# Four cross-attention layers on one core: two of eight subtractions move to GpSimd, one bank is ranked last, one product is issued later

## The chip, the core and the metric

The kernel runs on one core of a Trainium2 chip. The metric is device time in microseconds (us) of one execution, without the host. The kernel before takes 3668.16 us, the median of three runs (3667.93 to 3672.54).

## What is computed

Four cross-attention layers run one after the other on four batches. Layers 0, 2 and 3 are alike and are called *masked*: 16 heads of 64, and a bias on a few key columns, which comes from two masks over the queries. Layer 1 is called *grouped*: an RMS norm first, 16 query heads of 16, four key heads.

```python
# masked layer (0, 2, 3); x: (4, 512, 256), context: (4, 1024, 512)
q, k, v = x @ Wq, ctx @ Wk, ctx @ Wv           # 16 heads of 64
logits = einsum('bhqd,bhkd->bhqk', q, k) * 64 ** -0.5 + col_bias
out = einsum('bhqk,bhkd->bhqd', softmax(logits), v) @ Wo + bo + x
# grouped layer (1)
xn = x * rsqrt(mean(x * x) + 1e-5) * norm_w
scores = einsum('btgrd,bsgd->bgrts', q, k) * 0.25
out = einsum('bgrts,bsgd->btgrd', softmax(scores), v) @ wo + x
```

All data are float32.

## The kernel before, in words

**Units and steps.** The work of a layer and a batch is cut into eight units of two heads. There are 96 masked and 32 grouped units. A hand-written table (lines 57 to 64) gives every one of 96 steps one masked unit and, in 32 of them, a grouped one as well. The instruction order of all engines is written out in program order (`manual_schedule`); nothing is reordered afterwards. In the main loop (line 1029) a step `n` knows

- `g`, the masked unit whose logits are made in this step, and `g1`, that of the step before, whose product with the values is made now,
- `lam`, the grouped unit of this step, whose logits were already made in the step before,
- `coming`, the grouped unit of the next step, whose logits are made in this one.

The text calls a step with `coming` and without `lam` a *coming step* (there are 28: 11, 13, 15 ... 23, 27 ... 39 and so on), and one with `lam` a *lam step* (32, of which four, 24, 40, 56 and 72, also have a `coming`). Mostly the two kinds alternate.

**A masked unit.** `scores` (line 695) makes the logits, transposed: eight tiles of 128 keys by 1024 (two heads of 512 queries, one to each half of a tile). Each tile takes one pair of PSUM banks: TensorE multiplies (L704; every float32 product is two matmul records, so a tile has four), ScalarE copies the pair to SBUF (L714), and VectorE takes the running maximum of all eight in the first tile's pair (L718), the unit's `mx_place`. `max_quarters` (line 759) reduces that maximum (L755), gives `mx_place` back, and works on through L765 to L770 in a scratch bank of its own, `w`. `max_everywhere` spreads the result over a pair of banks, `mb` (L781). Then VectorE subtracts `mb` from the eight tiles (L789), ScalarE takes exponentials (L795), GpSimd adds the exponentials up (L834) in `g.mx`, a ninth slot in SBUF beside the unit's eight tiles. In the next step `attend` multiplies with the values (L734), and `normalise` divides (L755 on `st`, L859 to L880).

**A grouped unit.** In the step before, `logits_pair` (line 676) makes its logits in four pairs of tiles, spread between the projections of that step (L681 on TensorE, L687 on ScalarE, L693 on VectorE); after the fourth pair come `max_quarters` and `max_everywhere`, here into SBUF. In its own step GpSimd makes all eight subtractions (L787), before anything else of that step; ScalarE takes the exponentials, and `attend_grouped` (line 1180) makes the product, as one item of the list below.

**The fill list.** After `scores` and `attend`, a step has a list of projections (`fill`, lines 1162 to 1214), each with a cost in us, which TensorE works off while VectorE and ScalarE finish the softmax. The events (subtractions and exponentials, lines 1148 to 1154) are put between the items by these costs, whenever an item that returns a function has been issued. `attend_grouped` goes into the list where the costs ahead of it reach 9.5, and not ahead of an output projection of a grouped unit.

**Banks.** PSUM has eight banks, handed out at build time by `Place` (lines 99 to 121): a `Place(2)` takes the even-odd pair that has been returned longest ago, by a running number of returns, and a `Place(1)` the bank returned longest ago (preferring one whose neighbour is out). So the number written by `back()` decides which bank the next tiles get, and with it whose reads they wait for.

Of the kernel before, what the change touches and what calls it, by code (L numbers as in the profile page):

```python
# [12 lines left out]
ALU = mybir.AluOpType  # L13
# [7 lines left out]
NT = T // P  # L21
# [61 lines left out]
def kernel(ctx: ExitStack, tc: tile.TileContext, a: dict, out: bass.AP):  # L83
    nc = tc.nc
# [8 lines left out]
    def t_(shape, tag, name, bufs=1, dtype=FP):  # L93
        return sb.tile(shape, dtype, tag=tag, name=name, bufs=bufs)
# [40 lines left out]
    def give_set(g):  # L135
        sets_free.append(g.set)
# [501 lines left out]
    def reciprocal_rows(out_, in_, room):  # L638


        turned = room[:, 0:S]
        short = t_([P, S // 32, 1], "short", f"short{len(turns)}")
        turns.append(0)
        nc.vector.transpose(turned, in_)
        nc.vector.reciprocal(short, turned.rearrange("p (c r) -> p c r", r=32)[:, :, 0:1])
        nc.vector.transpose(
            out_.rearrange("p (c r) -> p c r", r=32), short.to_broadcast([P, S // 32, 32])
        )
# [75 lines left out]
    def attend(g, blocks=range(NT)):  # L724
        for t in blocks:
            for j in range(2):
                rows = g.rows[j]
                if not g.masked:
                    rows = slice(64 * g.h + 32 * j, 64 * g.h + 32 * (j + 1))
                at, first, last = rows, 0, NT - 1  # L730
                if not g.masked:
                    at = slice(64 * (t % 2) + 32 * j, 64 * (t % 2) + 32 * (j + 1))
                    first, last = t % 2, NT - 2 + t % 2
                nc.tensor.matmul(  # L734
                    g.po[at, :], lhsT=g.v[:, t, rows], rhs=g.st[t][:, j * S : (j + 1) * S],
                    start=(t == first), stop=(t == last),
                )
# [16 lines left out]
    def over_quarter(out_, of, op):  # L754
        nc.vector.tensor_reduce(  # L755
            out_, of.rearrange("p (b x) -> p b x", x=32), AX.X, op, apply_transpose=True
        )

    def max_quarters(g):
        w = Place(1)  # L760
        quarter, half = w.ap[:, 0:32], w.ap[0:64, 32:64]
        other = t_([64, 32], "other_max", f"other_max_{g.name}")
        over_quarter(quarter, g.mx_place.ap, ALU.max)
        g.mx_place.back()
        nc.vector.tensor_copy(other, quarter[64:128, :])  # L765
        nc.vector.tensor_tensor(half, quarter[0:64, :], other, ALU.max)
        nc.vector.tensor_copy(other[0:32, :], half[32:64, :])
        g.every = t_([P, 2 * S // 32, 1], "every", f"every_{g.name}")
        for h in range(4):
            nc.vector.tensor_tensor(  # L770
                g.every[32 * h : 32 * (h + 1), :, 0], half[0:32, :], other[0:32, :], ALU.max
            )
        w.back()

    def max_everywhere(g):
        if g.masked:
            g.mb_place = Place()
            g.mb = g.mb_place.ap
        else:
            g.mb = g.mx  # L780
        nc.vector.transpose(  # L781
            g.mb.rearrange("p (b r) -> p b r", r=32), g.every.to_broadcast([P, 2 * S // 32, 32])
        )

    def subtract(g, t):
        if not g.masked:
            nc.gpsimd.tensor_tensor(g.st[t], g.st[t], g.mb, ALU.subtract)  # L787
            return
        nc.vector.tensor_tensor(g.st[t], g.st[t], g.mb, ALU.subtract)  # L789
        if t == NT - 1:  # L790
            g.mb_place.back()

    def exponentials(g, t):
        st = g.st[t]
        nc.scalar.activation(st, st, AF.Exp)  # L795
        if t == 0 or not g.masked:
            return
        g.acc = g.mx
        if t < g.now:
            running_sum(g, t)  # L800
# [9 lines left out]
    def attend_last(g):  # L810

        place_out(g, 2)
        parts_of = [g.st[t] for t in range(g.now, NT)] + [g.acc]

        def add(n):
            for j in range(2):
                nc.tensor.matmul(
                    g.psum[g.rows[j], :], lhsT=ones[:, 0:64], rhs=parts_of[n][:, j * S : (j + 1) * S],
                    start=(n == 0), stop=(n == NT - g.now),
                )  # L820

        for t in range(NT):
            for j in range(2):
                nc.tensor.matmul(
                    g.po[g.rows[j], :], lhsT=g.v[:, t, g.rows[j]], rhs=g.st[t][:, j * S : (j + 1) * S],
                    start=(t == 0), stop=(t == NT - 1),
                )
            if t >= g.now:
                add(t - g.now)
        add(NT - g.now)  # L830
        g.ot = t_([P, S], "ot", f"ot_{g.name}", bufs=3)
# [41 lines left out]
    def normalise(g):  # L873
        w = Place(1)
        reciprocal_sums(g, w.ap)
        w.back()
        scale_out(g)
# [5 lines left out]
    def project_out(*of):  # L883

        g = of[0]
        x, acc = xs[g.l, g.b], xs.get((g.l + 1, g.b))
        opens = acc is None
        if opens and g.masked:
            acc = new_state(g.l + 1, g.b)
        elif opens:  # L890

            acc = xs[g.l + 1, g.b] = x
            x_at[g.l + 1, g.b] = x_at[g.l, g.b]
        w = Place()
        m = w.ap
        for k in range(KC):
            for each in of:
                nc.tensor.matmul(  # L898
                    m[:, k * S : (k + 1) * S], lhsT=each.wo[:, k * P : (k + 1) * P], rhs=each.ot,
                    start=each is g, stop=each is of[-1],  # L900
                )
        y = m.rearrange("p (k q) -> p k q", q=S)

        def add_last(q):
            nc.vector.tensor_tensor(acc[:, :, q], y[:, :, q], acc[:, :, q], ALU.add)

        def add():
            if g is masked[-1]:
                for i in range(0, NI, 2):
                    add_last(slice(i * P, (i + 2) * P))  # L910
                    store(g.b, range(i, i + 2))
                left[g.b] = -1
            elif opens and g.masked:
                bo = columns[f"L{g.l}_xattn_bo"]
                for k in range(KC):
                    nc.vector.scalar_tensor_tensor(
                        acc[:, k, :], y[:, k, :], bo[:, k : k + 1], x[:, k, :], ALU.add, ALU.add
                    )
            else:
                nc.vector.tensor_tensor(acc, y, x if opens else acc, ALU.add)  # L920
            w.back()

        left[g.b] -= len(of)
        return add
# [33 lines left out]
    def at(n):  # L958
        return steps[n] if 0 <= n < len(steps) else (None, None)
# [8 lines left out]
    def head(g):  # L968
        return steps[step_of[1, g.b, 0]][1]
# [59 lines left out]
    for n in range(len(steps) + 2):  # L1029
        g, lam = at(n)  # L1030
        follows, coming = at(n + 1)
# [99 lines left out]
        if g:  # L1131
            max_quarters(g)
            max_everywhere(g)
        if g1 and g:
            attend(g1)
            give_set(g1)
            if not ending:
                late.append(lambda: normalise(g1))
        elif g1:
            attend_last(g1)  # L1140
            adds = [project_out(*each) for each in outs]
            outs = []
            reciprocal_rows(g1.ot, g1.psum, g1.mx)
            scale_out(g1)
            for add in adds:
                add()
# [8 lines left out]
        if coming:  # L1155
# [6 lines left out]
        fill, of_grouped = (  # L1162
            [
                (1.8 * len(each), lambda each=each: project_out(*each))
                for each in outs if each[0].masked == m
            ]
            for m in (True, False)
        )
# [9 lines left out]
        if lam:  # L1178

            def attend_grouped():  # L1180
                while any(of is lam for _, of, _ in events):
                    events.pop(0)[2]()
                lam.v = head(lam).v
                place_out(lam)
                attend(lam)
                give_set(lam)
                late.append(lambda: keep_odd(lam))
                if lam.h == 1:
                    late.append(lambda: turn_grouped(lam))
                return lambda: keep_even(lam)  # L1190

            total, where = 0.0, 0
            first_at = max((fill.index(each) + 1 for each in of_grouped), default=0)
            while where < len(fill) and (total < 9.5 or where < first_at):
                total += fill[where][0]
                where += 1
            fill.insert(where, (3.6, attend_grouped))
# [79 lines left out]
```

## Time and profile before

| | |
|---|---|
| median of three runs | 3668.16 us |
| the profiled execution, its own time | 3666.02 us |
| its span, first to last instruction | 3664.2 us |
| TensorE matmul, busy | 3550.1 us (97%) |
| VectorE | 3019.4 us (82%) |
| ScalarE | 2317.6 us (63%) |
| GpSimd | 2219.7 us (61%) |
| one subtraction on VectorE (L789), 768 of them | 1215 ns |
| one subtraction on GpSimd (L787), 256 of them | 2376 ns |
| one copy of a pair of banks by ScalarE (L714), 768 | 1044 ns |
| granted TensorE clock, mean | 0.998 |

How to read it: the 97% does not say that TensorE streams all the time. A matmul that waits in the array, or runs beside another at less than full speed, counts as busy, too. A stall is better seen in the times at which the matmuls of one stage start. The `scores` of a step start with its first L704 matmul; that is taken as the start of the step. Step 17 starts at 642.1, step 18 at 682.7, step 19 at 722.6 us. Granted clock and DMA are no limit here (DMA moved 42 GB/s in the mean).

### The profile page before, as it was taken

To read this page: it belongs to the slowest core of one execution; us is meant where nothing else is said; L and a number is where in the kernel's file an instruction comes from. 1 tells how busy PE (TensorE), PEld (TensorE's weight loads), DVE (VectorE), ACT (ScalarE), POOL (GpSimd) and SP (SyncE) were. 2 spreads that over 40 slices of the span, in tenths; PEclk is the share of its full clock that TensorE was granted. 3 is DMA by queue.
4 is the path that set the end of the run, shared out by engine and by line. 5 is a ranking of instruction groups with operands and counts; after the bars stand their busy time and mean duration, and the time that the engine had idled before them with its cause. 6 is when DMAs were issued, how large, how long until landed. Compare 5 with 4: busy or idle time off the path is not lost.

```text
span 3664.2 us, 40591 instructions
## 1 busy us (share of the span) xinstructions
PE 3550.1 (97%) x14510; PEld 1719.1 (47%) x14510; DVE 3019.4 (82%) x4134; ACT 2317.6 (63%) x2657; POOL 2219.7 (61%) x1005
## 2 busy tenths in 40 slices
PE   8999999999999999999999999999999999999998
PEld 4554444444454444444444444444444445454454
DVE  7877788888878878897888889788878978888787
ACT  4556566666756666675666667566666765555554
POOL 3565466656746665684666658556765755545454
PEclk9999999999999999999999999999999999999999
DMA  3231101101021011102101110110002011002100
GB/s 88 61 118 53 55 28 41 31 18 51 19 67 42 26 30 48 57 19 61 49 26 28 55 51 19 53 56 27 28 28 72 19 32 49 18 26 72 32 29 8
DMA packets 164845, 154.69 MB, mean 42 GB/s; under 512 B 42776, under 2 KB 142616, under 8 KB 164132
## 3 DMA queue, kind: packets, MB, share of 16 engines
q1 hardware_dynamic: 158990, 139.00, 12.1%
q0 software_dynamic: 2560, 8.39, 0.7%
q10 hardware_dynamic: 3094, 4.72, 0.6%
q8 instruction: 114, 1.87, 0.2%
q14 instruction: 87, 0.71, 0.1%
HBM read 133.20 MB, written 14.68 MB: 40 GB/s over the span
## 4 chain that ended last, share of the span: by engine, by line
PE 76%; DVE 15%; ACT 6%; issue 2%; ACTq 0%; DMA 0%; DVEq 0%; POOL 0%; POOLq 0%
PE ps L734 16%; PE ps L526 16%; PE ps L565 15%; PE ps L704 15%; PE ps L898 4%; PE ps L622 4%; PE ps L681 4%; DVE ps L718 4%; DVE st L789 3%; ACT st L795 3%; DVE ps L755 2%; DVE ps L693 2%; ACT st L714 2%; ACT st L687 1%; DVE ps L781 1%
## 5 line engine op out<-in xcount | busy, mean ns | idle before, releaser
L834 POOL TENSOR_TENSOR st<-st 128x1024 f32<-128x1024 f32 x668 | 1579.6, 2365 | 1112.6 <-ACT st L795 1067.7
L795 ACT ACTIVATE st<-st 128x1024 f32<-128x1024 f32 x1024 | 1038.3, 1056 | 570.2 <-DVE st L789 499.6
L718 DVE TENSOR_TENSOR ps<-ps,st 128x1024 f32<-128x1024 f32 x672 | 827.6, 1232 | 384.0 <-ACT st L714 323.3
L789 DVE TENSOR_TENSOR st<-st,ps 128x1024 f32<-128x1024 f32 x768 | 881.2, 1215 | 3.3
L734 PE MATMUL ps<-st,v 128*64 128x512 f32 (+1 forms) x4064 | 802.1, 596 | 8.5 <-ACT st L795 8.5
L704 PE MATMUL ps<-qt,kt 64*128 64x512 f32 x3072 | 732.8, 604 | 75.4 <-DVE ps L755 45.2
L714 ACT COPY st<-ps 128x1024 f32<-128x1024 f32 x768 | 718.8, 1044 | 128.4 <-PE ps L710 64.3
L787 POOL TENSOR_TENSOR st<-st 128x1024 f32<-128x1024 f32 x256 | 596.8, 2376 | 295.3 <-DVE st L781 295.3
L526 PE MATMUL ps<-ctx,wk 128*128 128x512 f32 x1536 | 692.4, 600 | 2.2 <-ACT ctx L428 2.2
L565 PE MATMUL ps<-wv,ctx 128*128 128x256 f32 x3072 | 682.3, 381 | 0.0
L565 PEld LDWEIGHTS ps<-wv,ctx 128*128 128x128 f32 x3072 | 581.5, 190 | 130.6 <-issue 53.5
L704 PEld LDWEIGHTS ps<-qt,kt 64*128 64x128 f32 x3072 | 315.6, 187 | 434.9 <-issue 130.3
L734 PEld LDWEIGHTS ps<-st,v 128*64 128x64 f32 (+1 forms) x4064 | 242.2, 130 | 545.0 <-issue 432.3
L526 PEld LDWEIGHTS ps<-ctx,wk 128*128 128x128 f32 x1536 | 285.7, 191 | 394.0 <-issue 369.4
L693 DVE TENSOR_TENSOR ps<-ps,st 128x1024 f32<-128x1024 f32 x224 | 276.1, 1232 | 86.8 <-ACT st L687 75.4
L687 ACT COPY st<-ps 128x1024 f32<-128x1024 f32 x256 | 247.0, 1015 | 87.0 <-PE ps L681 86.6
L572 ACT COPY v<-ps 128x512 f32<-128x512 f32 x192 | 110.5, 576 | 150.9 <-PE ps L565 150.6
L628 ACT ACTIVATE qt<-ps 128x512 f32<-128x512 f32 x96 | 56.6, 590 | 220.2 <-PE ps L622 220.2
L622 PE MATMUL ps<-x,wq 128*128 128x512 f32 x384 | 188.1, 613 | 1.1 <-ACT x L391 1.1
L681 PE MATMUL ps<-qt,kt 32*128 32x512 f32 x1024 | 171.5, 640 | 8.0 <-DVE o L748 5.2
L898 PE MATMUL ps<-ot,wo 128*128 128x512 f32 x384 | 177.9, 606 | 0.7 <-DVE ot L880 0.7
L531 ACT COPY kt<-ps 128x512 f32<-128x512 f32 x192 | 110.8, 577 | 101.5 <-PE ps L526 97.2
(142 smaller groups left out, 1696.4 us busy)
## 6 DMA issues: line engine op xcount, KB each, us to landing
ctx<-kept SPq DMA_DIRECT2D x30, 1024.0 KB, 8.0
wk<-in_L_xattn_Wk_dram SPq DMA_DIRECT2D x47, 512.0 KB, 3.6
wv<-in_L_xattn_Wv_dram SPq DMA_DIRECT2D x47, 512.0 KB, 3.7
wq<-in_L_xattn_Wq_dram SPq DMA_DIRECT2D x96, 128.0 KB, 3.5
wo<-in_L_xattn_Wo_dram SPq DMA_DIRECT2D x96, 128.0 KB, 3.9
st<-kept SPq DMA_DIRECT2D x4, 2048.0 KB
kept<-st SPq DMA_DIRECT2D x12, 512.0 KB, 3.2
qt<-qt ACTq DMA_DIRECT2D x32, 128.0 KB, 2.2
```

The costliest lines, as they stand in the source:

```text
L526: nc.tensor.matmul(m, lhsT=g.w["k"][:, k, :], rhs=ctx_half[g.b, n][:, k, :], start=(k == 0), stop=(k == KT - 1),)
L565: nc.tensor.matmul(m[:, half * 2 * P : (half + 1) * 2 * P], lhsT=ctx_half[g.b, t // 4][:, k, t % 4 * P : (t % 4 + 1) * P], rhs=g.w["v2"][: ...
L622: nc.tensor.matmul(m, lhsT=g.wq[:, k, :], rhs=x[:, k, :], start=(k == 0), stop=(k == KC - 1))
L693: nc.vector.tensor_tensor(top, top, g.st[t], ALU.max)
L704: nc.tensor.matmul(m[:, j * S : (j + 1) * S], lhsT=g.kt[g.rows[j], keys], rhs=g.qt[g.rows[j], :], start=True, stop=t > 0,)
L714: nc.scalar.copy(g.st[t], m)
L718: nc.vector.tensor_tensor(top, top, g.st[t], ALU.max)
L734: nc.tensor.matmul(g.po[at, :], lhsT=g.v[:, t, rows], rhs=g.st[t][:, j * S : (j + 1) * S], start=(t == first), stop=(t == last),)
L787: nc.gpsimd.tensor_tensor(g.st[t], g.st[t], g.mb, ALU.subtract)
L789: nc.vector.tensor_tensor(g.st[t], g.st[t], g.mb, ALU.subtract)
L795: nc.scalar.activation(st, st, AF.Exp)
L834: nc.gpsimd.tensor_tensor(g.acc, g.st[0] if t == 1 else g.acc, g.st[t], ALU.add)
```

## The change

It has three parts.

- **A.** In the 28 coming steps two of the eight masked subtractions (tiles 6 and 7) are made by GpSimd. GpSimd's operand is in SBUF, so ScalarE first copies `mb` from PSUM into `g.mx`, which the running sum overwrites afterwards. The copy and the two subtractions are issued right after `max_everywhere`. `mb` is given back after VectorE's last subtraction, now that of tile 5.
- **B.** In `max_quarters` the pair `mx_place` of a *grouped* unit is given back with a return number that is higher by six. `Place` then ranks it behind the banks that are returned after it.
- **C.** In lam steps without a `coming`, `attend_grouped` goes into the fill list where the costs ahead of it reach 13.0, and no longer 9.5.

```diff
@@ max_quarters
-        g.mx_place.back()
+        g.mx_place.back(0 if g.masked else 6)
@@ subtract
+        if t >= g.here:
+            return
         nc.vector.tensor_tensor(g.st[t], g.st[t], g.mb, ALU.subtract)
-        if t == NT - 1:
+        if t == g.here - 1:
             g.mb_place.back()
+
+    def subtract_aside(g):
+        nc.scalar.copy(g.mx, g.mb)
+        for t in range(g.here, NT):
+            nc.gpsimd.tensor_tensor(g.st[t], g.st[t], g.mx, ALU.subtract)
@@ main loop
             max_quarters(g)
             max_everywhere(g)
+            g.here = NT - 2 if coming and not lam else NT
+            if g.here < NT:
+                subtract_aside(g)
@@ attend_grouped's place
-            while where < len(fill) and (total < 9.5 or where < first_at):
+            while where < len(fill) and (total < (9.5 if coming else 13.0) or where < first_at):
```

## The prediction

> **What bounds the kernel now.** I read the page's busy shares first, then the list of who waited for whom, then the timeline around the start of one lam step.
>
> ```profile
> PE 3550.1 (97%) x14510; PEld 1719.1 (47%) x14510; DVE 3019.4 (82%) x4134; ACT 2317.6 (63%) x2657; POOL 2219.7 (61%) x1005
> ```
>
> TensorE (PE) is busy by far the longest, so relief for VectorE (DVE) counts only where TensorE waits for it. From the list of waits (who waited, for whom, total us, times, longest; PEld are TensorE's weight loads):
>
> ```profile
> PE ps L704 <- DVE ps L755: 45.2, 28, 2.1
> PE ps L704 <- ACT st L687: 27.4, 24, 1.2
> PE ps L734 <- ACT st L795: 8.5, 10, 1.2
> ```
> ```profile
> PEld ps L704 <- DVE every L770: 8.7, 28, 0.3
> ```
>
> The logits (L704) wait 28 times for the reduction L755: once in each lam step but the first of each batch (12, 28, 44, 60). The timeline where step 17 ends and step 18 begins (start, duration, engine, line; in brackets the idle time before and its releaser):
>
> ```profile
> 681.62 1.93 ACT L687 COPY st<-ps 128x1024 f32<-128x1024 f32 x2 [0.54 <-PE ps L681]
> 682.66 2.57 DVE L693 TENSOR_TENSOR ps<-ps,st 128x1024 f32<-128x1024 f32 x2 [0.61 <-ACT st L687]
> 682.68 1.13 PE L704 MATMUL ps<-qt,kt 64*128 64x512 f32 x4 [1.14 <-ACT st L687]
> ...
> 683.86 1.02 PE L704 MATMUL ps<-qt,kt 64*128 64x512 f32 x4
> ...
> 685.27 1.26 DVE L755 TRANSPOSE_TENSOR_REDUCE ps<-ps 128x32 f32<-128x1024 f32 x1
> ...
> 686.59 6.02 PE L704 MATMUL ps<-qt,kt 64*128 64x512 f32 x24 [1.70 <-DVE ps L755]
> ...
> 687.23 0.76 DVE L770 TENSOR_TENSOR every<-ps,other_max 32x32 f32<-32x32 f32 x4
> ...
> 689.27 4.68 ACT L714 COPY st<-ps 128x1024 f32<-128x1024 f32 x5 [0.45 <-PE ps L704]
> ```
>
> Tiles 0 and 1 start at 682.68 and 683.86, tile 2 at 686.59, when the grouped L755 has ended. The next stage (L734) starts at 692.54, so the logits took 9.86 us. Where nothing waits (step 19, from 722.63 to 729.92) they take 7.29. So 2.57 us are lost in each of these 28 steps.
>
> **B, the banks.** I followed `Place` by hand through both versions. Before, step 18 takes, tile by tile: the pair of the coming step's last even logits, that of its last odd logits, the grouped `mx_place` (waits for L755), and a fourth pair, one bank of which was `max_quarters`' scratch `w`. That scratch is read last by L770. After, `mx_place` ranks last, so the fourth pair becomes third. Tile 2 then waits not for L755 (ends 686.53) but for L770 (ends 687.99), later in the same DVE chain. In this case at tile 2 only the half on the scratch bank waits. The trace of before shows that this wait is real: the 28 PEld waits for L770 are tile 3's, which was held only 0.3 us, having started late.
>
> Further, `mx_place` now comes up only at tile 7 (or, in some steps, not at all), so tiles 1 to 6 alternate between two pairs and not three. Worked through for step 18: tile 2's second half starts at 688.05. Before, tile 3's second half started then and its copy at 689.27, that is 1.22 later; copies take 0.94 each (4.68/5), a tile of matmuls 0.86 (four records, two at a time, 0.43 apart). So after: tile 2's copy 689.27 to 690.2; tile 3 688.9 to 689.8, copy to 691.1; tile 4 needs tile 2's pair, 690.25, copy 691.5 to 692.4; tile 5 691.2, copy to 693.3; tile 6 needs tile 4's pair, 692.45; tile 7 693.3 to 694.2; L734 at about 694.35. That is 1.8 us later than 692.54: 0.86 for the tile that slipped, the rest for two pairs in place of three. VectorE's maxima hide nothing of it: L734 follows on TensorE at once, and what TensorE loses there stays lost, since its later items in the step wait for nothing else (C's stall apart). All 28 have this order of banks: 28 x 1.8 = +50. The four first lam steps had no wait, but also get fewer pairs in rotation: tile 3 waits 0.6 for tile 1's copy, +2.4. Two plain steps, 26 and 42, start on other banks, freed sooner, about -0.7 each; in six coming steps (29, 39, 45, 55, 61, 71) a logits tile now gets banks that wait for the key copy L531, about +0.3 each. These cancel.
>
> **C, the later product.** Timeline of step 18, TensorE:
>
> ```profile
> 710.09 3.63 PE L734 MATMUL ps<-st,v 128*32 128x512 f32 x28
> 714.55 1.05 PE L734 MATMUL ps<-st,v 128*32 128x512 f32 x4 [0.83 <-ACT st L795]
> ```
>
> The grouped product runs from 710.09 to the next L565 at 715.53: 5.44 us, against 3.57 in step 16. It waits for the last grouped exponentials. In twelve lam steps the starts show this (1.9 to 2.2 us in ten, 1.0 in two: 46 and 54), together 21 us. Listed two value items later, each some 1.7 us (L565: 7.1 us for four), it arrives 3.4 us later by itself and 1.8 more by B, after the exponentials: all 21 go. What stands behind it is late but has cover: the copy L744 and the divisions L748 to L851 ended at 721.7 in step 18, the next step's first maximum starts at 726.0. C: -21.
>
> **A, the subtractions.** Removed: 28 x 2 x 1.215 = 68 us of DVE. Added: 28 copies of 1.04 on ACT (as L714), 56 subtractions of 2.37 on POOL (as L787), 133 us. The timeline of step 17:
>
> ```profile
> 660.62 2.19 ACT L795 ACTIVATE st<-st 128x1024 f32<-128x1024 f32 x2 [9.63 <-DVE st L789]
> ...
> 662.89 9.68 POOL L834 TENSOR_TENSOR st<-st 128x1024 f32<-128x1024 f32 x4 [16.45 <-ACT st L795]
> ...
> 663.90 5.74 DVE L789 TENSOR_TENSOR st<-st,ps 128x1024 f32<-128x1024 f32 x5
> ...
> 667.71 3.02 ACT L795 ACTIVATE st<-st 128x1024 f32<-128x1024 f32 x3
> ...
> 670.64 0.57 ACT L531 COPY kt<-ps 128x512 f32<-128x512 f32 x1
> ```
>
> The ACT copy waits for L781 (ends 659.33), runs to 660.4 and fits in the idle 9.63; the first exponential queues behind it, but waits for the first subtraction until 660.6 anyway. POOL subtracts from 660.5 to 665.3, ahead of ACT's use at 669; the seven sums behind it end 2.4 us later (682.2 for 679.8), before POOL's next job at 689.4. So the added work is hidden. But what is gained? TensorE's first pair of grouped logits waits for L531, and L531 for ACT's three exponentials in a row, bound by ACT itself. The later maxima (L693) wait for L687, not for earlier DVE work (0.61 before the last two, above). So the chain L687, L693, L755, L770 ends when it did. A: 0. If DVE set the end, -68; if the copies stood on the path, +29. The rows stand at nothing. If an ACT copy were no longer covered, 1.04 us a step.
>
> [...] L789 in step 18 takes 9.15 us for eight beside a working POOL, in step 17 3.48 for three beside an idle one: 1.14 and 1.16 each, no slowing. [...]
>
> **Sum.** 3666.0 (the profiled execution) + 50 + 2 - 21 + 0 = 3697 or 3698. The median of the runs lies 2.1 above that execution, so 3700 us, 0.9% slower.
>
> **Rivals.**
>
> - *DVE's chain ends earlier after all* (faster). If A lets L770 end 2.43 us sooner, tile 2 starts at 685.6 and L734 at 691.9, 0.6 before now: 28 x -0.6 - 21 + 2 = -36, 3632. It turns faster from about 1.1 us of advance, where B costs 0.7 a step and C pays it. For it: DVE is freed shortly before L693 begins. Against it: the waits of L693 for L687.
> - *Only the slipped tile costs* (no change). If two pairs in rotation are enough, B is 28 x 0.86 = 24, and with C's -21 the sum is +3 to +5: 3672.
> - *The halves fall out of step* (much slower). In steps 46, 54 and 68 the logits took 1.7 to 1.9 us more than in the other 25: a half that was released alone ran in turn with its neighbour, not beside it. Now a lone half is the rule at tile 2. If it happens in all, 28 x 1.7 = 48 on top: 3748. For the main case: in 25 of 28 it did not.
>
> **How the numbers follow.** Main case 0.62 (its own range 3680 to 3722: B from 1.2 to 2.6 a step), out of step 0.12, no change 0.11, faster 0.15. Range 3650 to 3740: from half of the faster case's gain to most of the out-of-step case; A's far ends, -68 and +29, are kept out beyond that, since no wait in the rows points to them. A measurement of this kernel can tell about 0.2% (7 us) from no change. Chances: faster 0.14, same 0.11, slower 0.75.
>
> **What would show it.** Right: the waits of L704 for L755 gone, and about 28 waits for L770 of some 3 us in their place; L704 in lam steps 11.5 to 11.7 us; no wait of L734 for L795; coming steps as long as before, with six L789 each. Wrong: L755 and L770 earlier after the last L687 than now, shorter coming steps, or tile 2 starting without a wait.

## The result and the profile after

| kernel | median of runs, us | lowest to highest | ratio to before, 95% interval |
|---|---|---|---|
| before, beside the changed kernel | 3668.05 | 3664.66 to 3672.54 | 1 |
| changed (A, B and C) | 3756.61 | 3756.32 to 3760.72 | 1.0243 [1.0226, 1.0261] |

The change makes the kernel 2.4% slower. The sign was forecast; the size, 3700, was not, and 3756.61 lies above the range. The profiled execution took 3760.72 us, its span is 3758.9 (3664.2 before): 94.7 us more.

The page of the changed kernel, busy times:

```profile
PE 3617.8 (96%) x14510; PEld 1708.6 (45%) x14510; DVE 2960.2 (79%) x4078; ACT 2340.8 (62%) x2685; POOL 2350.7 (63%) x1061
```

VectorE has lost 59 us of work, GpSimd has gained 131 with the 56 moved subtractions. (The prediction's 68 for VectorE multiplies the 1.215 us of one; subtractions in a row overlap a little: the five at 663.90 in step 17 of before took 5.74 us, 1.148 each.) TensorE does the same 14510 matmuls, but is busy 67.7 us longer: stalled or slower matmuls, not more of them.

The changed kernel's list of waits (who waited, for whom, total us, times, longest):

```profile
PEld ps L704 <- DVE every L770: 90.2, 28, 4.3
...
PE ps L704 <- DVE every L770: 67.1, 28, 3.5
...
DVE st L791 <- ACT st L796: 30.2, 28, 1.1
...
PE ps L681 <- ACT kt L531: 15.2, 28, 0.9
```

The waits of the logits for L755 are gone. Waits for L770 stand in their place, as the prediction said of part B. The third line was not foreseen. (Part A adds seven lines to the code: the subtraction is now L791, ScalarE's copy L796, GpSimd's subtraction L798, the exponential L802.)

The third line in the timeline of the changed kernel, step 17 (which starts at 650.0; start, duration, engine, line, in brackets the idle time before and its releaser):

```profile
665.59 1.26 DVE L781 STREAM_TRANSPOSE ps<-every 128x1024 f32<-128x1024 f32 x1
666.89 1.01 ACT L796 COPY st<-ps 128x1024 f32<-128x1024 f32 x1 [8.02 <-DVE ps L781]
667.93 3.48 DVE L791 TENSOR_TENSOR st<-st,ps 128x1024 f32<-128x1024 f32 x3 [1.08 <-ACT st L796]
667.98 4.70 POOL L798 TENSOR_TENSOR st<-st 128x1024 f32<-128x1024 f32 x2 [15.65 <-ACT st L796]
669.19 2.19 ACT L802 ACTIVATE st<-st 128x1024 f32<-128x1024 f32 x2 [1.29 <-DVE st L791]
```

L781 has written the maxima into `mb` at 666.85. VectorE idles 1.08 us until ScalarE has read the same `mb`. In step 17 of the kernel before, L781 ended at 659.33 and VectorE went on without a pause:

```profile
659.37 3.48 DVE L789 TENSOR_TENSOR st<-st,ps 128x1024 f32<-128x1024 f32 x3
```

The first exponential, and all that hangs on it, moves by about as much.

The start of lam step 18 in the changed kernel:

```profile
692.35 1.88 PE L704 MATMUL ps<-qt,kt 64*128 64x512 f32 x6
692.56 1.93 ACT L714 COPY st<-ps 128x1024 f32<-128x1024 f32 x2 [0.52 <-PE ps L710]
...
693.76 1.26 DVE L755 TRANSPOSE_TENSOR_REDUCE ps<-ps 128x32 f32<-128x1024 f32 x1
...
695.73 0.77 DVE L770 TENSOR_TENSOR every<-ps,other_max 32x32 f32<-32x32 f32 x4
...
696.55 6.77 PE L704 MATMUL ps<-qt,kt 64*128 64x512 f32 x18 [2.32 <-DVE every L770]
```

The second half of tile 2 starts at 696.55, when L770 has ended, and not after L755. From there to the next stage, at 704.10, 22 matmuls take 7.55 us (the last line shows the first 18 of them). In step 24 of the same kernel the same 22 took 6.38. The windows view of step 18 shows why (window, its length, then the busy times of PE, PEld, DVE, ACT and POOL, the granted TensorE clock, DMA share, GB/s):

```profile
691.20:697.10 5.90, 3.58 (x14) 1.43 (x16) 5.55 (x11) 2.76 (x3) 0.00 (x0) 1.00 0.59 154
697.10:700.50 3.40, 3.40 (x10) 1.40 (x6) 3.03 (x3) 1.61 (x2) 2.58 (x2) 0.51 0.01 2
```

For 3.4 us after the wait the clock is half; step 24 has no such stretch. In the kernel before, the same view of step 46, one of the three odd steps of the prediction's third rival:

```profile
1823.40:1826.80 3.40, 3.40 (x10) 2.65 (x9) 3.29 (x3) 1.56 (x2) 2.25 (x1) 0.50 0.00 0
```

Half clock there, too. The clock records hold 3 such stretches before (10.2 us in all) and 29 after (36 windows of 3.413 us, 122.9 us; the one at the very end, 6.5 us before and 5.6 after, left out). Of the 29, 25 lie in the logits of lam steps and four in the coming steps 27, 29, 39 and 59. So the sentence ahead of the prediction, that the granted clock is no limit, holds for the kernel before alone, and there but for these 10 us.

**Where the 94.7 us are**, by the starts of the stages in both traces: +87.3 in the logits of the 32 lam steps (28 of them from 9.95 to 12.98 us in the mean, the four others from 7.3 to 7.9); +35.4 in the coming steps, between their first grouped logits and their end; -20.8 at the grouped product; -7.1 in small ones (-5.5 at L565 in lam steps with a `coming`, -1.6 in steps 26 and 42).

### The profile page after: what moved, and what is told of

It reads as the page before. It is cut to its first block, busy times and chain, and to the rows that moved or that the text cites. A ratio compares the mean times of both kernels' runs of the same rounds, so it can differ in the third digit from the quotient of the medians.

```text
span 3758.9 us, 40578 instructions
## 1 busy us (share of the span) xinstructions
PE 3617.8 (96%) x14510; PEld 1708.6 (45%) x14510; DVE 2960.2 (79%) x4078; ACT 2340.8 (62%) x2685; POOL 2350.7 (63%) x1061
## 4 chain that ended last, share of the span: by engine, by line
PE 71%; DVE 18%; ACT 7%; issue 3%; DMA 0%; DVEq 0%; ACTq 0%; POOL 0%; POOLq 0%
PE ps L565 18%; PE ps L734 15%; PE ps L704 13%; PE ps L526 12%; DVE ps L718 7%; PE ps L622 4%; PE ps L681 4%; DVE st L791 4%; ACT st L802 3%; PE ps L905 3%; DVE ps L755 2%; DVE ps L693 2%; ACT st L714 2%; DVE every L770 1%; DVE ps L781 1%
## 5 line engine op out<-in xcount | busy, mean ns | idle before, releaser
L841 POOL TENSOR_TENSOR st<-st 128x1024 f32<-128x1024 f32 x668 | 1578.9, 2364 | 672.3 <-ACT st L802 625.3
L802 ACT ACTIVATE st<-st 128x1024 f32<-128x1024 f32 x1024 | 1027.8, 1054 | 276.4 <-DVE st L791 255.0
L704 PE MATMUL ps<-qt,kt 64*128 64x512 f32 x3072 | 789.9, 634 | 103.8 <-DVE every L770 67.1
L791 DVE TENSOR_TENSOR st<-st,ps 128x1024 f32<-128x1024 f32 x712 | 817.4, 1213 | 32.6 <-ACT st L796 30.2
L734 PE MATMUL ps<-st,v 128*64 128x512 f32 (+1 forms) x4064 | 789.8, 595 | 0.0
L787 POOL TENSOR_TENSOR st<-st 128x1024 f32<-128x1024 f32 x256 | 596.3, 2372 | 269.4 <-DVE st L781 269.4
L565 PE MATMUL ps<-wv,ctx 128*128 128x256 f32 x3072 | 683.5, 380 | 0.0
L565 PEld LDWEIGHTS ps<-wv,ctx 128*128 128x128 f32 x3072 | 580.4, 190 | 135.2 <-issue 55.9
L704 PEld LDWEIGHTS ps<-qt,kt 64*128 64x128 f32 x3072 | 304.8, 195 | 530.7 <-ACT st L714 199.1
L798 POOL TENSOR_TENSOR st<-st 128x1024 f32<-128x1024 f32 x56 | 131.8, 2376 | 429.7 <-ACT st L796 429.7
L687 ACT COPY st<-ps 128x1024 f32<-128x1024 f32 x256 | 249.5, 1016 | 88.4 <-PE ps L681 88.3
L681 PE MATMUL ps<-qt,kt 32*128 32x512 f32 x1024 | 189.2, 645 | 15.4 <-ACT kt L531 15.2
```

What stands on the lines that cost most here:

```text
L565: nc.tensor.matmul(m[:, half * 2 * P : (half + 1) * 2 * P], lhsT=ctx_half[g.b, t // 4][:, k, t % 4 * P : (t % 4 + 1) * P], rhs=g.w["v2"][: ...
L681: nc.tensor.matmul(ws[odd].ap[:, j * S : (j + 1) * S], lhsT=g.kt[rows, i * P : (i + 1) * P], rhs=g.qt[rows, :], start=True, stop=True,)
L704: nc.tensor.matmul(m[:, j * S : (j + 1) * S], lhsT=g.kt[g.rows[j], keys], rhs=g.qt[g.rows[j], :], start=True, stop=t > 0,)
L734: nc.tensor.matmul(g.po[at, :], lhsT=g.v[:, t, rows], rhs=g.st[t][:, j * S : (j + 1) * S], start=(t == first), stop=(t == last),)
L841: nc.gpsimd.tensor_tensor(g.acc, g.st[0] if t == 1 else g.acc, g.st[t], ALU.add)
```

## The experiments

**Theory.** A costs about 1 us in each of 28 coming steps, because two engines read `mb` and the program makes one wait for the other (1.08 us in step 17). B costs the 1.8 us a step that was worked out, and besides makes gaps in TensorE's work after which its clock is granted at half. C is worth its 21 us. **Rivals.** GpSimd's work slows VectorE (A); the two pairs in rotation cost much more than was worked out (B); halves that run in turn (the prediction's third rival) explain the slow steps, not the clock.

The parts alone, then the fill, then A taken apart, then B mended. The first four were timed against the same runs of before, as were the four after them.

### A alone

`max_quarters` and the place of `attend_grouped` as before; the hunks `subtract`, `subtract_aside` and the main loop as in the change.

> Part A alone (copy on ScalarE, two subtractions on GpSimd), banks and list as before. Theory (the ScalarE copy and VectorE's subtractions may not read the same banks of mb at once, so VectorE starts 1.08 us later, and with it the exponentials, L531 and the first pair of grouped logits): each of 28 coming steps 1.0 to 1.3 us longer, +28 to +36 us; lam steps unchanged. Rival 1 (my prediction: A is covered): 0 within 7 us. Rival 2 (VectorE's relief is worth something by itself, the loss of the changed kernel is all B's): 10 us or more faster.

Measured: 3701.2 us, ratio 1.0092 [1.0075, 1.0109]; 35.1 us of it in the coming steps, nearly all that the changed kernel loses there. The commonest difference of a coming step is 0.97 or 0.98, 27 us for all 28; nearly all the rest is half clock in steps 39, 55 and 71 (1.7 to 2.0 us each) and another 0.5 us in each of six steps (see the table further down). Part A is no free part.

### B alone

```diff
-        g.mx_place.back()
+        g.mx_place.back(0 if g.masked else 6)
```

> Part B alone. Theory (tile 2 waits for L770, two pairs rotate, and the longer idle time makes the clock gate grant half speed for 3.4 us in nearly every lam step): L704 in lam steps 5.0 to 5.9 us over its unhindered time in place of 2.8, +80 to +90 us, and 25 or more stretches at half clock where before had 3. Rival (waits as predicted, without the clock): 4.6 over, +53 us.

Measured: 3737.3 us, ratio 1.0186 [1.0169, 1.0203]: +69 (its span +74.2), between the rival and the expectation. It has 19 stretches of half clock in the lam steps, and not 25 or more. The logits of the lam steps lost 87, as in the changed kernel; 9.4 came back at the grouped product, which now started later by itself, and some 4 elsewhere. The windows view of two lam steps, 18 and 16, of this kernel:

```profile
691.60:703.50 11.90, 9.03 (x36) 3.02 (x36) 11.13 (x16) 7.36 (x8) 5.19 (x3) 1.00 0.23 72
608.90:622.80 13.90, 11.58 (x36) 4.35 (x36) 11.64 (x16) 7.44 (x8) 7.20 (x4) 0.75 0.10 34
```

Both windows are the whole logits of their step, the same 34 matmul records in the same order of banks (x36 counts two of the next stage): 11.9 us at full clock, 13.9 where two windows of 3.4 us ran at half. 11.9 is 2.1 above before; the prediction had 1.8. Nine of the 28 lam steps kept their clock; all nine took 11.86 to 11.92. In steps 18 and 16 alike tile 2's second half is released alone, so it isn't the lone half that makes a step slow, and the third rival of the prediction falls.

### C alone

```diff
-            while where < len(fill) and (total < 9.5 or where < first_at):
+            while where < len(fill) and (total < (9.5 if coming else 13.0) or where < first_at):
```

> Part C alone. Theory and prediction: the waits of the grouped product for its exponentials go, -21 us, all of it in twelve lam steps. Rival (the step's end or the next step's start is late instead): between -10 and +5 us.

Measured: 3639.78 us, ratio 0.9924 [0.9908, 0.9941], faster than both kernels. The grouped product gains 20.8 us by the traces. The median gains 28: the span of this trace is 24.9 lower, with 2.2 in the logits, where one stretch of half clock fewer is found. The rest fits the clock too: its four executions were granted 0.999 in the mean, the seven of before beside them 0.995 to 0.999. In the changed kernel's step 18 the product runs from 725.11 to 728.68, 3.57 us (5.44 before).

### The changed kernel with its gaps filled

While tile 2 waits for its second half, TensorE repeats the product of the first half, whose bank is free. This is extra work of 256 matmul records; the values stay as they are.

```diff
-            for j in range(2):
+            order_of = [0, 1]
+            if scratch and scratch[0] in w.banks:
+                order_of = [1 - (scratch[0] - w.banks[0])] * 5 + [scratch[0] - w.banks[0]]
+                scratch.pop()
+            for j in order_of:
```

> The changed kernel, with TensorE kept at work where it waits for L770 and only one half of tile 2 is held by the scratch bank: the other half's product is made five times over in the same bank (same values). Theory (clock gate): TensorE is idle under 1.5 us there, half-speed stretches fall from about 28 to under 8 and the kernel becomes 20 to 35 us faster than the changed one although it computes more. Rival (a half that is released alone runs in turn with its neighbour, whatever the clock): no gain, or slower by the added products; the spacing of 0.85 us stays.

Measured: 3740.68 us, ratio 1.0197 [1.018, 1.0214]: 16 us faster than the changed kernel with more to do, and below the 20 expected. The half-clock stretches fell from 29 to 6, and in the logits of the lam steps from 25 to none; the six lie in coming steps. Step 18 of this kernel, most of the stretch of its logits (692.39 to 704.18; windows view), and the matmuls in it (timeline; the scores are L710 here):

```profile
692.40:702.90 10.50, 10.03 (x38) 4.15 (x40) 9.84 (x15) 6.41 (x7) 3.76 (x2) 1.00 0.33 87
```
```profile
693.57 6.18 PE L710 MATMUL ps<-qt,kt 64*128 64x512 f32 x20
700.03 2.04 PE L710 MATMUL ps<-qt,kt 64*128 64x512 f32 x8 [0.28 <-ACT st L720]
```

The wait for L770 is covered by matmuls, and the clock stays at 1.00. The logits of the 28 lam steps sum to 331.3 us (363.4 in the changed kernel, 278.6 before). So 32 us of B's loss went with the gaps, and 53 stayed, which is close to the 50 of the prediction for these steps. The saving of the whole is smaller because the fill is no gain in the four other lam steps, where tile 3 hardly waited: they got 13.6 us longer.

### Only the copy

```diff
@@ main loop of the kernel before
+            if coming and not lam:
+                nc.scalar.copy(g.mx, g.mb)
```

> The kernel before with nothing added but ScalarE's copy of the maxima in the coming steps (28 x 1.04 us of ScalarE work; nobody reads the copy, and VectorE keeps all eight subtractions). My theory: VectorE's first subtraction waits until that copy has read the same PSUM bank, so the whole loss of part A is in the copy alone: a wait of VectorE for ScalarE 28 times, the first product of grouped logits about 1.0 to 1.2 us later in each coming step, 28 to 36 us slower than before (3696 to 3704), as with part A alone. [...] Rival 2: the copy only holds up ScalarE's own exponentials: they waited 9.6 us idle in step 17 before, so 0 as well.

Measured: 3702.0 us, ratio 1.0094 [1.0078, 1.0111], the time of A alone (3701.2). Waits, then step 17's timeline, of this kernel (L1135 is the copy):

```profile
DVE st L789 <- ACT st L1135: 30.2, 28, 1.1
```
```profile
661.12 1.26 DVE L781 STREAM_TRANSPOSE ps<-every 128x1024 f32<-128x1024 f32 x1 [0.46 <-DVE every L770]
662.41 1.01 ACT L1135 COPY st<-ps 128x1024 f32<-128x1024 f32 x1 [8.38 <-DVE ps L781]
...
663.46 3.48 DVE L789 TENSOR_TENSOR st<-st,ps 128x1024 f32<-128x1024 f32 x3 [1.08 <-ACT st L1135]
```

The copy's result is used by nobody, and VectorE waits for it all the same. The wait stands in the program: in all 28 coming steps VectorE's first subtraction waits here (30.2 us in all) for a semaphore that ScalarE raises, and in the kernel before for one of VectorE's own. In 24 of the 28 coming steps the step is 1.04 to 1.06 us longer, the length of the copy and its hand-over; the other four are +1.3 to +3.1, three of them with a half-clock stretch inside. 28 x 1.04 is 29 of the 35.2 us. So the loss isn't in the moved subtractions, which this kernel doesn't have, and rival 2 (0) falls.

### GpSimd's work without the copy

The maxima are not copied; GpSimd subtracts a constant, which leaves out the true scaling of two tiles in each coming step. The rest is A alone.

```diff
     def subtract_aside(g):
-        nc.scalar.copy(g.mx, g.mb)
+        nc.gpsimd.memset(g.mx, 30.0)
```

> Part A alone, but GpSimd subtracts a constant 30.0 that it sets itself in place of the maxima: ScalarE's copy is left out, and the last two tiles of each coming step are scaled by another number, so the output isn't the reference's. GpSimd still does its two subtractions of 2.4 us in each coming step, VectorE does six. My theory: the copy was the only cost and VectorE's relief is worth nothing, so 0, from -7 to +7 us against before. Rival 1: GpSimd's work beside VectorE costs by itself: +15 to +36. Rival 2: VectorE's relief of 2.4 us a step is worth something once the copy is gone: -14 to -68.

Measured: 3667.77 us, ratio 1.0001 [0.9991, 1.0011]. The groups of this kernel (busy and mean ns of one, then the idle time before them and what ended it):

```profile
L791 DVE TENSOR_TENSOR st<-st,ps 128x1024 f32<-128x1024 f32 x712 | 817.3, 1213 | 3.3
...
L798 POOL TENSOR_TENSOR st<-st 128x1024 f32<-128x1024 f32 x56 | 130.7, 2354 | 216.1 <-DVE ps L718 216.1
```

GpSimd does all its 56 subtractions (130.7 us). VectorE has hardly any idle time before its own (3.3 us over all 712; 32.6 with the copy) and needs 1213 ns for each (1215 before). GpSimd's two have no copy to wait for, so they run earlier than in part A, beside VectorE's reduction of the maxima (655.46 to 660.12 in step 17; VectorE's first subtraction starts at 660.89). How subtractions run beside each other is seen in the changed kernel: the 84 of VectorE that ran beside a moved one (the first of each three from 0.05 us ahead of it) took 1216 ns each. So GpSimd's work costs nothing, and VectorE's relief of two subtractions a step is worth nothing (19 of the 28 coming steps changed by -0.06 to -0.08 us; the six of 29, 39, 45, 55, 61 and 71 got 0.4 to 0.8 longer, three others 0.4 shorter, +0.4 in all). The loss of about 1 us in each coming step is the wait for the copy.

### B mended: the scratch out of the banks

Here part C stays, and part A is left out. In the first kernel the maxima's banks are ranked later by 6, as in part B:

```diff
-        w = Place(1)
-        quarter, half = w.ap[:, 0:32], w.ap[0:64, 32:64]
+        if g.masked:
+            w = Place(1)
+            room = w.ap
+        else:
+            room = t_([P, 64], "room_max", f"room_max_{g.name}")
+        quarter, half = room[:, 0:32], room[0:64, 32:64]
...
-        g.mx_place.back()
+        g.mx_place.back(0 if g.masked else 6)
...
-        w.back()
+        if g.masked:
+            w.back()
```

> Parts B and C as in the changed kernel, with one difference: the grouped maximum's scratch lies in SBUF, not in a PSUM bank. My theory of part B: the loss comes from tile 2 getting the scratch's bank, which L770 reads last; without it the same late ranking of the maxima's banks should gain: no wait for L755 or L770 at tile 2, the logits of a lam step 1 to 2.5 us shorter than in the kernel before (two pairs in rotation cost some of it), so with the later product 3575 to 3620 us, and the clock at full speed nearly everywhere. Rival (it is the ranking itself, two pairs of banks in place of three, that costs): no gain over before from part B, 3650 to 3690 us.

Measured: 3609.11 us, ratio 0.9839 [0.9822, 0.9855]. The second kernel differs in one number, `1.5` in place of `6`:

> The kernel before with the later grouped product, the grouped maximum's scratch in SBUF and not in a PSUM bank, and the grouped maxima's banks ranked later by only 1.5. By the order of banks the logits' first three tiles of a lam step then take banks that nothing late reads, and the maxima's banks come at the fourth tile, about when L755 has read them. My theory: the wait of tile 2 is gone whichever instruction it was for, about 2.5 us less in each of 28 lam steps (-70), and with the later product's -21 to -28 some 3570 to 3590 us; idle gaps of TensorE stay below those of before, so the clock stays at full speed nearly everywhere. Rival 1 (the maxima's chain sets the end of the logits in any case, whichever tile waits): only the later product's gain, 3635 to 3650. Rival 2 (VectorE is slower on SBUF scratch, or the maxima end later): 3650 or more.

Measured: 3597.95 us, ratio 0.9807 [0.9791, 0.9824], the fastest of all, though short of the 3570 to 3590 expected: the logits gave 38 us, the coming steps 29, since tile 0 of the next step no longer waits, and the grouped product 20, but 21 were given back at other stages of the lam steps. Step 18 with rank 1.5:

```profile
677.44 1.13 PE L704 MATMUL ps<-qt,kt 64*128 64x512 f32 x4
...
678.65 2.04 PE L704 MATMUL ps<-qt,kt 64*128 64x512 f32 x8
...
681.24 1.25 DVE L755 TRANSPOSE_TENSOR_REDUCE room_max<-ps 128x32 f32<-128x1024 f32 x1
...
681.40 3.99 PE L704 MATMUL ps<-qt,kt 64*128 64x512 f32 x16 [0.70 <-ACT st L714]
```

and with rank 6, matmuls alone:

```profile
678.46 2.04 PE L704 MATMUL ps<-qt,kt 64*128 64x512 f32 x8
...
681.21 2.05 PE L704 MATMUL ps<-qt,kt 64*128 64x512 f32 x8 [0.70 <-ACT st L714]
...
683.50 2.05 PE L704 MATMUL ps<-qt,kt 64*128 64x512 f32 x8 [0.25 <-ACT st L714]
...
685.80 1.13 PE L704 MATMUL ps<-qt,kt 64*128 64x512 f32 x4 [0.25 <-ACT st L714]
```

In both, tiles 1 and 2 follow without a wait for the maxima, and tile 0 no longer waits 1.14 us for L687 (its banks are now those of a key product). The logits of a lam step took 8.74 us with rank 1.5 and 9.62 with rank 6 (most steps). The difference, 0.88, is the price of two pairs in rotation: the waits of 0.25 for ScalarE's copies. The prediction had put it at 0.94. Without the late bank at tile 2 the late ranking itself is no loss against before.

### The scratch out of the banks, no later ranking

> The later grouped product and the grouped maximum's scratch in SBUF, with the banks of the maxima given out as in the kernel before: no later ranking at all. It tells which of the two edits of the run with rank 1.5 brought its 70 us. My theory: the scratch out of the banks is what counts, because the order of the pairs in a lam step then starts with one that nothing late reads (no wait of tile 0 for L687, 1.1 us a step) and L755 is met at the fourth tile: 3590 to 3605, within 8 us of the run with rank 1.5, and faster than rank 6 (3609). Rival: the ranking by 1.5 is needed to keep the maxima's banks off tile 2, and the scratch alone leaves the wait for L755: 3625 to 3645.

The edit is that of the last kernels without the number in `back`. Measured: 3619.75 us (3608.37 to 3625.37), ratio 0.9855 [0.9831, 0.9878], outside 3590 to 3605. My theory was half wrong: tile 0's wait went (the coming steps got 29.4 us shorter in sum, 29.1 with rank 1.5), but the pair of the maxima came up at tile 3 before L755 had ended. Its steps 18 and 48, timeline:

```profile
683.46 4.56 PE L704 MATMUL ps<-qt,kt 64*128 64x512 f32 x20 [1.84 <-DVE room_max L755]
```
```profile
1874.30 6.26 PE L704 MATMUL ps<-qt,kt 64*128 64x512 f32 x20 [1.84 <-DVE room_max L755]
```

The same gap of 1.84 us, the same 20 matmuls, and 4.56 us against 6.26. Of its 24 steps with this gap (2.2 in one) 13 hold a stretch of half clock, step 48 among them (0.53 granted from 1874.6 to 1878.0), step 18 doesn't. Rank 1.5 leaves a gap of 0.70 and had no such stretch in the whole span.

## Why the prediction was wrong

By terms, against the 94.7 us of the traces:

| term | predicted | measured | from |
|---|---|---|---|
| A, the copy | 0 | +27 | 28 x 0.97, the commonest difference of a coming step |
| B, order of banks | +52 | about +55 | the logits in the run with filled gaps (53 in 28 steps), and 2.4 in the four first lam steps |
| half clock | 0 | about +38 | 363.4 - 331.3 in the logits, some 5.5 in the coming steps 27, 29, 39 and 59 |
| C | -21 | -20.8 | grouped product |
| six coming steps (29, 39, 45, 55, 61, 71) | +1.8 | about +3 | 0.5 each; so in A alone, and not in B alone, where the prediction had it |
| small ones | -1.4 | -7 | -1.6 in steps 26 and 42; -5.5 at L565, as in B alone |

- **A, the step that failed: "So the added work is hidden."** The prediction asked only what is queued behind the copy on ScalarE, and found the exponential idle there. It didn't ask who else uses the copy's operand. `mb` lies in PSUM and VectorE reads it at the same moment; its first subtraction waits until the copy is done, 1.08 us, and the exponentials, the key copy L531 and the first grouped logits move with it. The price stood in the text ("if the copies stood on the path, +29") and was kept out of the range "since no wait in the rows points to them". No row of before could: there `mb` had one reader. The 28 waits of 1.08 us behind a copy that nobody needs, on a semaphore of ScalarE, show VectorE's read of `mb` held back until ScalarE's read of it has ended. Whether it is the bank or the tile that counts was not tried: all of these reads are of one tile.
- **A, what was right.** VectorE's relief is worth nothing, and VectorE is not slowed beside GpSimd: 1216 ns for the 84 subtractions that ran beside the moved ones, against 1215 in the kernel before.
- **B, right in mechanism and at full clock.** Tile 2 waits for L770, 28 times, and step 24, which kept its clock, took 11.76 us (9.85 before), in the forecast 11.5 to 11.7 but for 0.06. Both halves of the working hold: 0.88 a step for two pairs in place of three. Not all 28 steps are alike, as the prediction took them: in 25, 41, 57 and 73 the logits took 9.17 before and not 9.86.
- **B, what was missing: the clock.** The sum has no term for a clock that drops behind a longer gap, and that term measured about +38. The prediction saw the three odd steps 46, 54 and 68, 1.7 us longer, and put them down to halves that run in turn, with the argument "in 25 of 28 it did not". All three hold a window of half clock. The cause it named was wrong, and the base rate was taken from steps with gaps of 1.14 and 1.70 us, though the change's own working makes the second one about a microsecond longer (2.32 in the trace). The rival's price of 1.7 a step came near to half a window (3.413 / 2) for that reason, and 12 in 100 was too small a chance. A look at the granted clock in windows of those three steps would have told it.
- **C, right.** It is the one part that gains, 28 us alone.
- **The range** ended at 3740. A's 27 and the clock's 38 were both outside of it; either alone, on top of the 3697 or 3698 of the sum, would have ended inside it or at its end.

## What to carry over

Before handing part of a tile's work to another engine, list who else reads its PSUM operand at that moment: here a copy of 1.01 us on an idle engine stood on the path through the engine that was to be relieved, 1.08 us in each of 28 steps. When a wait of TensorE gets longer, price the clock as well as the wait (here the half-clock stretches went from 3 to 29, about 38 us), and look at the granted clock of the few steps that already run long. When banks are ranked by hand, follow each bank to its last reader; here taking a scratch out of PSUM turned a loss of 69 us into a gain of 31 beside C (3639.78 to 3609.11), and the smaller rank to 42.

## What the runs showed of the hardware

- The half-clock stretches start on one grid: in the changed kernel at 529.8, 615.1 and 697.0 us, which are 25 and 24 times 3.413 us apart, and last 3.413 us (22 of the 29) or 6.827 (7). Gaps of 1.70 to 2.05 us were followed by one in 3 of 24 lam steps (before), gaps of 1.84 to 2.2 in 13 of 24 (the last run), and gaps of 2.3 to 3.5 in 23 of 24 (the changed kernel).
- The length of one gap doesn't decide it. The six stretches that are left in the kernel with filled gaps follow gaps of 0.6 to 0.9 us among the grouped logits of coming steps, and gaps up to 1.4 us in the steps of the two mended kernels were followed by none. How much idle time it takes, the runs don't settle: the same gap of 1.84 us was followed by half clock in step 48 of the last run and not in step 18, and why the two differ was not shown.
- With one such stretch inside (step 48 of the last run), the same 20 matmuls took 6.26 us and not 4.56 (step 18).
- Executions of the kernel with gaps of 1.84 spread over 17 us (3608.37 to 3625.37), those of the two kernels with gaps of 0.70 over 0.7. The granted clock goes with it: 0.999 in the execution of 3608.37, 0.996 in that of 3614.17, 0.993 in the two of 3625. Only one of the four was traced, and why they differ was not shown.
